# Attention's planned matmuls gathered into every second step, with array shapes counted by the planner

## The chip, the cores and the metric

The kernel runs on one core of one Trainium2 chip. The metric is device time in microseconds (us) of that core; the time before is 1631.56 us, the median of three runs (1630.38 to 1631.83). A profile is one further execution, taken with the hardware profiler.

## The reference

Four sequences of 1024 tokens with 256 channels, all in float32, pass one layer of attention and one mixture of experts:

```
x = x + layernorm(attention(layernorm(x)))   # 16 heads of 16, RoPE on q and k, softmax
x = x + layernorm(moe(layernorm(x)))         # 8 experts, the 2 farthest by distance
                                             # to a centroid, weights softmaxed
```

An expert is silu(x Wg + bg) * (x W1 + b1), times W2, plus b2, with 684 hidden channels. Attention's scores are q k / 4, and its softmax runs over all 1024 keys of a sequence.

## The kernel before, in words

The program has three parts: a start (to about 74 us), attention's steps (to about 1022 us) and the experts (the rest, with a short tail for the last layernorm). The change is in the second.

**Units and steps.** Heads are taken in groups of four. A unit is one sequence, one group of heads and one half of the queries (512); there are 32 units, in the list `order`. A unit has 8 steps, one for each 128 keys, so there are 256 steps, written out by `step(n)` (L709). A step does on TensorE (PE):

- `scores` for two pairs of heads (L723): four products of keys and queries into `sc` (L730), on 64 rows of the array, and four small products that add the negative row maximum `shift` (L736). ScalarE (ACT) takes exp of each into `e` (L740).
- up to three `peaks` (L701), usually two, of a later unit: each is two products `pm` (L645), also on 64 rows, whose row maxima VectorE (DVE) takes into `part` (L648). They run some 12 steps ahead (LEAD, L791). When a unit's maxima are complete, DVE makes `mx` of them (L619 to 624), PE transposes it into `pmx` (L628), and ACT copies that to `shift` (L632).
- `weighted` (L799): the product of the step before's `e` with the values, four matmuls `av` (L805), each on 32 columns of the array.
- then up to QUOTA (L790) planned parts, in the loop of L780.

**Planned parts.** Everything else that attention's part must do is a `Work` (L406): a generator that yields the cost of its next piece and then writes it out. "P540 A550" says that the piece takes 540 ns of PE and then 550 of ACT; D is DVE, G GpSimd (POOL), W a wait only. The Works that use PE put a whole 128 x 128 array to use: transposes `pt`, `ps`, `po`, `ptm`, `pd`, and products `pp`, `pv`, `py`, `pdist`, `rank`. Among them, for the next sequence, `prepare` (L461) normalizes x and `project` (L494) makes q and k (`pp`, copied by ACT to `turned`, L508); `split` (L555) turns q and k by their positions on POOL (`rot`, `sw`) and cuts them into a high and a low half (`split`); `stack` (L565) transposes these (`ps`, L572), copies them by ACT (`half`, L580), and SyncE's queue (SP) copies them by DMA into the tiles `stack` (L592) that pm and sc read.

**The order.** PE, DVE, ACT and SP run their instructions in the order in which the Python program writes them out, and `pool` keeps POOL's in that order too. The program decides it by a plan: `free` holds, for each engine, the time up to which it believes it to be taken. `run_one` (L452) takes the first Work by due time whose next piece fits. A piece fits (L417) when the Works it comes after have been written out to their end, its own time `ready` has come, and no engine would be taken too far ahead (ROOM). `finish` (L446) writes out a Work at once, whether it fits or not; it is called when its result is needed, as for `shifts[u]` at a unit's first step. The plan adds 230 ns of PE for a pair of pm (L705), 460 for a pair of heads' sc (L742), and 1200 for a step's av (L809); a change of the array's shape has no cost of its own in it.

**Banks.** sc and most of the planned parts share a ring of four PSUM banks, which ACT empties; pm, pmx, pd, py, pdist and rank share a ring of three, which DVE mostly empties.

Of the kernel before, what the change touches and what calls it, by code (L numbers as in the profile page):

```python
# [16 lines left out]
P = 128  # L17
# [40 lines left out]
def sandwich(  # L58
# [22 lines left out]
    def bank(name, pool=ps1):  # L81
        return pool.tile([P, TB], F32, tag="bank", name=name)
# [217 lines left out]
    for e in range(NE):  # L300
        for w, to, cols in (
            (wg, 0, slice(0, FF)), (w1, FF, slice(FF - (P - R2), FF)), (w1, FF + P - R2, slice(0, NC * P))
        ):
            n = cols.stop - cols.start
# [84 lines left out]
    free = dict.fromkeys("PDAG", 0)  # L389
# [4 lines left out]
    def bank_free(r, n):  # L394
        return max(ring[r][(taken[r] + i) % len(ring[r])] for i in range(n))

    def take(r, until):
        ring[r][taken[r] % len(ring[r])] = until
        taken[r] += 1

    ROOM = dict(P=10**9, D=1400, A=2600, G=15000)
    LAG = dict(P=280, D=120, A=150, G=200, W=0)
    at_step = [0]
# [2 lines left out]
    class Work:  # L406
# [10 lines left out]
        def fits(self):  # L417
# [6 lines left out]
            if self.ready > (now if first in "PW" else max(now, free[first])):  # L424
                return False
            return all(e == "W" or free[e] + c - now <= ROOM[e] for e, c in costs)

        def run(self):
            t = self.ready
            bank_used = self.need[0] == "P"  # L430
            if bank_used:
                r = self.costs()[1][0]
                t = max(t, bank_free(r, 1))
            for i, (e, c) in enumerate(self.costs()):
                if e != "W":
                    t = max(t, free[e], free["P"] - 300)
                    free[e] = t + c
                t += c + LAG[e]
                if bank_used and i == 1:
                    take(r, t)  # L440
            self.ready = t
            self.need = next(self.gen, None)
            if self.need is None:
                works.remove(self)
# [7 lines left out]
    def run_one(first="PADGW"):  # L452

        w = next((w for w in works if w.need[0] in first and w.fits()), None)
        if w:
            w.run()
        return w
# [198 lines left out]
    def outputs(u, av):  # L656

        b, g, qb = order[u]
        ou = ap2.tile([P, TB], F32, tag="ou", name=f"ou_{u}")
        nc.scalar.copy(ou, av)  # L660
        free["A"] = max(free["A"], free["P"] + 300) + 550
        av_free[0] = free["A"] + LAG["A"]

        def turn_back():
            yield "P500 D750"
            if g == 0:
                old = divmod(b * NQB + qb - 3, NQB)
                if old in closing:
                    closing[old].finish()
                outs[b, qb] = cl.tile(  # L670
                    [P, NTB, NH, HD], F32, tag="outs", name=f"outs_{b}_{qb}", bufs=3
                )
            pd = bank(f"pd_{u}")
            for i in range(NTB):
                nc.tensor.transpose(
                    pd[:, i * P : (i + 1) * P], ou[:, i * P : (i + 1) * P], ident
                )

            by = pd.rearrange("p (t j d) -> p t j d", j=4, d=32)
            rec = small.tile([P, NTB, 4], F32, tag="rec", name=f"rec_{u}")  # L680
            nc.vector.reciprocal(rec, by[..., HD])
            nc.vector.tensor_tensor(
                outs[b, qb][:, :, 4 * g : 4 * g + 4, :], by[..., :HD],
                rec[..., None].to_broadcast([P, NTB, 4, HD]), ALU.mult,
            )

        back = Work(turn_back(), at_step[0] + 5)
        backs.append(back)
        back.ready = av_free[0]
        if g == NG - 1:  # L690

            before_ = list(settling.values())
            closing[b, qb] = Work(
                finish(b, qb), at_step[0] + 6,
                after=[back] + late + [closing[k] for k in closing] + before_[:-1],
            )
            settling[b, qb] = Work(
                settle(b, qb), at_step[0] + 8, after=[closing[b, qb]] + before_
            )

    def peaks():  # L701
        for _ in range(2):
            free["D"] = max(free["D"], free["P"] + 500) + 605
            take("D", free["D"] + LAG["D"])
        free["P"] += 230  # L705
        drawn[0] += 1
        next(tops)

    def step(n):  # L709

        u, kb = n // NT, n % NT
        at_step[0] = n
        b, g, qb = order[u]
        if kb == 0:
            shifts[u].finish()
        es = []
        if bulk and (n % 3 < 2 if n < 53 else n > 60):
            to, of = bulk.pop(0)  # L720
            nc.sync.dma_start(out=to, in_=of)

        def scores(pr):  # L723
            q, k_ = stacks[b, g, qb][pr][0], stacks[b, g, kb // NTB][pr][1]
            kt = kb % NTB * P
            scs = []
            for s in range(2):
                r = slice(64 * s, 64 * s + 64)
                sc = bank(f"sc_{n}_{pr}_{s}", pssc)
                nc.tensor.matmul(  # L730
                    sc, k_[r, kt : kt + P], q[r], start=True, stop=False
                )
                scs.append(sc)
            for s in range(2):
                r = slice(64 * s, 64 * s + 64)
                nc.tensor.matmul(  # L736
                    scs[s], bring[pr][r, :], shift[u][r, :], start=False, stop=True
                )
                e = ap1.tile([P, TB], F32, tag="e", name=f"e_{n}_{pr}_{s}", bufs=8)
                nc.scalar.activation(e, scs[s], AF.Exp, scale=1.0 / HD**0.5)  # L740
                es.append(e)
            free["P"] += 460  # L742
            for s in range(2):
                free["A"] = max(free["A"], free["P"] + 300) + 485
                take("A", free["A"] + LAG["A"])

        def when(kind):
            if kind == "M":
                return bank_free("D", 2)
            if kind == "V":  # L750
                return max(weighted_ready[0], av_free[0] if waiting[0][1] == 0 else 0)
            return bank_free("A", 2)

        lead = min(LEAD, NT + n // 4)
        share = max(0, min(3, 2 * (n + lead) - drawn[0], len(order) * UNIT - drawn[0]))
        todo = ["M"] * min(share, 1) + [0, 1] + ["M"] * (share - 1)
        while todo:
            kind = next((k for k in todo if when(k) <= free["P"] + 100), None)
            if kind == 1 and 0 in todo:
                kind = 0  # L760
            if kind is None:
                if set(todo) == {"M"} and drawn[0] > 2 * (n + NT + 2):
                    break
                if run_one("ADGW"):
                    continue
                kind = min(todo, key=when)
                if kind == 1 and 0 in todo:
                    kind = 0
            free["P"] = max(free["P"], when(kind))
            todo.remove(kind)  # L770
            if kind == "M":
                peaks()
            else:
                scores(kind)
            while run_one("ADGW"):
                pass
        if waiting:
            free["P"] = max(free["P"], when("V"))
            weighted(*waiting.pop(0))
        for i in range(QUOTA):  # L780
            while run_one("ADGW"):
                pass
            if not run_one("P"):
                break
        while run_one("ADGW"):
            pass
        waiting.append((u, kb, es))
        weighted_ready[0] = free["A"] + LAG["A"]

    QUOTA = 2  # L790
    LEAD = 12  # L791
    UNIT = 4 * NTB
    shifts, closing, settling, backs = {}, {}, {}, []
# [5 lines left out]
    def weighted(u, kb, es):  # L799
        b, g, qb = order[u]  # L800
        if kb == 0:
            avs[u] = psav.tile([P, TB], F32, tag="av", name=f"av_{u}")
        av = avs[u]
        for j in range(4):
            nc.tensor.matmul(  # L805
                av[32 * j : 32 * j + 32, :], v_aug[kb][:, 4 * g + j, :], es[j],
                start=(kb == 0), stop=(kb == NT - 1),
            )
        free["P"] += 1200  # L809
        if kb == NT - 1:  # L810
            outputs(u, av)

# [612 lines left out]
    def open_pool(key, stack, **kw):  # L1425
        room[key] = stack.enter_context(tc.tile_pool(name=key, reuse_waits="tile", **kw))
# [11 lines left out]
    def make_room():  # L1438
        attn.close()
        beside[0] = True  # L1440
        ROOM.update(D=3000, A=3500)
        open_pool("psu", behind, bufs=5, space=PSUM)
# [14 lines left out]
    with tc.manual_schedule(engines={ET.SP, ET.PE, ET.DVE, ET.Activation}):  # L1457
# [24 lines left out]
        while waiting:  # L1482
            weighted(*waiting.pop(0))
# [134 lines left out]
```

## Time and profile before

| | us |
|---|---|
| median of three runs | 1631.56 |
| the profiled execution's own time | 1639.77 |
| its span, first to last instruction | 1638.0 |
| attention's steps, 74 to 1022 | 948.0 |
| PE busy in them | 917.1 |
| DVE busy in them | 746.3 |
| ACT busy in them | 681.3 |
| POOL busy in them | 362.3 |

In the trace, a float32 product appears as two matmuls (a step's four av as eight). PE's rows give the time from the start of a group's first matmul to the modelled end of its last, and neighbouring groups overlap a little, so the time of a piece is better read from start to start. A row ends with the idle time of its engine before it, in brackets, and with what ended that. The mean granted clock of PE is 0.976 of full speed over the span, and 1.00 in the steps.

### The profile page before, as it was taken

What the parts mean: (1) busy time and instruction counts of PE and PEld (TensorE: products, weight loads), DVE (VectorE), ACT (ScalarE), POOL (GpSimd) and SP (SyncE); (2) the same over time, 40 slices, a digit from 0 to 9 for tenths busy, and PEclk for the clock granted to TensorE, in tenths of its full rate; (3) what the DMA queues carried; (4) which work ended last, traced back from release to release, by engine and by line L of the source; (5) the groups of instructions that cost most, each with busy time, mean ns of one, the idle gap of its engine ahead of it and who ended that gap; (6) DMA issues with size and microseconds to landing.
All of it is one profiled execution on the core that took longest, in us unless ns stands there. A gap on an engine that the chain in (4) does not pass through costs nothing. (4 is left out here: it accounts for less than half of the span.)

```text
span 1638.0 us, 27716 instructions
## 1 busy us (share of the span) xinstructions
PE 1532.8 (94%) x9456; PEld 1004.4 (61%) x9456; DVE 1046.5 (64%) x2511; ACT 854.8 (52%) x1754; POOL 513.2 (31%) x951
## 2 busy tenths in 40 slices
PE   7889999999999999999999999999999999999960
PEld 4444455645545554445554444788888888899950
DVE  4686788787788787868788883434434433334348
ACT  3366777677777767767677667322311111222213
POOL 6652152254372344462243112133230111111100
PEclk9899999999999999999999999999999999999985
DMA  4299887246054232212141042145455555788855
GB/s 121 90 247 237 236 237 186 85 117 177 12 132 136 75 103 80 53 52 65 37 94 40 1 159 87 66 167 203 179 183 195 195 194 221 251 312 300 304 226 199
DMA packets 114036, 247.94 MB, mean 151 GB/s; under 512 B 16772, under 2 KB 76967, under 8 KB 108007
## 3 DMA queue, kind: packets, MB, share of 16 engines
q1 hardware_dynamic: 103287, 215.47, 42.1%
q0 software_dynamic: 9120, 26.38, 4.9%
q10 hardware_dynamic: 1488, 4.33, 0.7%
q8 instruction: 75, 1.23, 0.3%
q14 instruction: 66, 0.54, 0.1%
HBM read 149.18 MB, written 80.73 MB: 140 GB/s over the span
## 5 line engine op out<-in xcount | busy, mean ns | idle before, releaser
L648 DVE TENSOR_REDUCE part<-pm 128x1 f32<-128x512 f32 x1024 | 640.5, 683 | 134.1 <-PE pm L645 132.1
L740 ACT ACTIVATE e<-sc 128x512 f32<-128x512 f32 x1024 | 530.2, 604 | 149.0 <-PE sc L736 147.5
L1330 PE MATMUL pu<-xT,w 128*128 128x256 f32 (+3 forms) x2024 | 359.9, 333 | 2.4 <-DMA w<-wall 1.2
L1330 PEld LDWEIGHTS pu<-xT,w 128*128 128x128 f32 (+1 forms) x2024 | 313.7, 190 | 33.2 <-issue 1.6
L1336 ACT ACTIVATE sil<-pu,w 128x256 f32<-128x256 f32 (+3 forms) x276 | 117.1, 425 | 415.9 <-PE pu L1330 392.9
L645 PE MATMUL pm<-stack,stack 64*128 64x512 f32 x992 | 282.5, 465 | 15.0 <-DVE part L648 11.9
L805 PE MATMUL av<-e,v 128*32 128x512 f32 x2048 | 274.9, 606 | 0.3 <-ACT e L740 0.3
L1341 DVE SCALAR_TENSOR_TENSOR h<-pu,w,sil 128x256 f32<-128x256 f32 (+1 forms) x230 | 97.2, 423 | 221.5 <-ACT sil L1336 220.6
L645 PEld LDWEIGHTS pm<-stack,stack 64*128 64x128 f32 x992 | 136.5, 185 | 162.1 <-DVE part L648 111.1
L730 PE MATMUL sc<-stack,stack 64*128 64x512 f32 x992 | 220.1, 405 | 4.1 <-ACT half L580 3.6
L736 PE MATMUL sc<-shift,bring 64*128 64x512 f32 x1024 | 222.7, 398 | 0.5 <-ACT shift L632 0.2
L1377 POOL DMA_INDIRECT res<-yo,ids x71 | 68.8, 969 | 411.7 <-DVE yo L1376 406.3
L1364 PE MATMUL pe<-w,h 128*128 128x256 f32 x710 | 167.5, 383 | 0.0
L1364 PEld LDWEIGHTS pe<-w,h 128*128 128x128 f32 x710 | 132.6, 190 | 25.4 <-issue 8.3
L730 PEld LDWEIGHTS sc<-stack,stack 64*128 64x128 f32 x992 | 113.8, 186 | 37.9 <-ACT e L740 15.0
L736 PEld LDWEIGHTS sc<-shift,bring 64*128 64x128 f32 x1024 | 105.7, 185 | 21.4 <-ACT shift L632 5.2
L1376 DVE TENSOR_SCALAR yo<-pe,xt 128x256 f32<-128x256 f32 x71 | 34.4, 484 | 90.3 <-PE pe L1364 90.2
L805 PEld LDWEIGHTS av<-e,v 128*32 128x32 f32 x2048 | 40.8, 108 | 71.1 <-issue 65.5
L992 POOL DMA_INDIRECT rows<-xr,to x64 | 62.6, 978 | 55.9 <-DVE to L987 34.6
L139 POOL TENSOR_TENSOR t_y<-y_y 128x4 f32<-128x4 f32 x24 | 4.7, 197 | 182.2 <-DVE y_y L334 181.0
L503 PE MATMUL pp<-wqk,nT 128*128 128x512 f32 (+1 forms) x128 | 61.1, 604 | 0.0
L139 POOL TENSOR_TENSOR rot<-turned,bias_qk 128x512 f32<-128x512 f32 x30 | 39.2, 1307 | 67.0 <-ACT turned L508 66.9
(297 smaller groups left out, 1396.2 us busy)
## 6 DMA issues: line engine op xcount, KB each, us to landing
w<-wall SPq DMA_DIRECT2D x46, 2034.0 KB
rows<-empty SPq DMA_DIRECT2D x35, 1032.0 KB
stack<-half SPq DMA_DIRECT2D x186, 128.0 KB
stack<-half SPq DMA_DIRECT2D x124, 64.0 KB
xt<-rows SPq DMA_DIRECT2D x25, 258.0 KB
wall<-in_wg_dram SPq DMA_DIRECT2D x16, 342.0 KB
wall<-in_w_dram SPq DMA_DIRECT2D x16, 320.0 KB
wall<-in_w_dram SPq DMA_DIRECT2D x8, 640.0 KB
```

The costliest lines, as they stand in the source:

```text
L645: nc.tensor.matmul(pm, q[r, i * P : (i + 1) * P], k_[r], start=True, stop=True)
L648: nc.vector.tensor_reduce(part[:, i, 2 * pr + s, half : half + 1], pm, AX.X, ALU.max)
L730: nc.tensor.matmul(sc, k_[r, kt : kt + P], q[r], start=True, stop=False)
L736: nc.tensor.matmul(scs[s], bring[pr][r, :], shift[u][r, :], start=False, stop=True)
L740: nc.scalar.activation(e, scs[s], AF.Exp, scale=1.0 / HD**0.5)
L805: nc.tensor.matmul(av[32 * j : 32 * j + 32, :], v_aug[kb][:, 4 * g + j, :], es[j], start=(kb == 0), stop=(kb == NT - 1),)
L992: sent = nc.gpsimd.indirect_dma_start(out=rows[:, :], out_offset=bass.IndirectOffsetOnAxis(ap=to[:, i, t : t + 1], axis=0), in_=xr[:, t, i ...
L1330: nc.tensor.matmul(pu[:m, i, :n], w[:, c0 : c0 + m], xT[:, k, :n], start=(k == 0), stop=(k == KC - 1),)
L1336: nc.scalar.activation(sil[:m, :n], pu[:m, 0, :n], AF.Silu, bias=w[:m, OB + f : OB + f + 1])
L1341: nc.vector.scalar_tensor_tensor(h[:, f, :n], pu[:, 1, :n], bias, sil[:, :n], ALU.add, ALU.mult)
L1364: nc.tensor.matmul(po[:, :C], hs[j % 2][:, f, i * P : (i + 1) * P], w[:, O2 + f * C : O2 + (f + 1) * C], start=False, stop=(f == NC - 1),)
L1377: sent = nc.gpsimd.indirect_dma_start(out=res[:, :], out_offset=bass.IndirectOffsetOnAxis(ap=ids, axis=0), in_=y, in_offset=None,)
```

## The change

The planned parts of a step are taken in even steps only, and then up to four instead of two. The planner keeps the shape in which it last left the array (128, 64 or 32) and adds PE time when a piece needs another: 225 ns for a change to 64, 210 to 32, 150 to 128. In return av costs 860 instead of 1200. The costs of a plain step in the plan are thus 230 x 2 + 460 x 2 + 860 + 225 + 210 = 2675 instead of 2580. No instruction is added or removed; all four engines' orders are decided anew.

```diff
+    shape = [0]
+
+    def array(rows_):
+
+        if rows_ != shape[0]:
+            free["P"] += {64: 225, 32: 210, P: 150}[rows_]
+            shape[0] = rows_
+
...
             if bank_used:
+                array(P)
                 r = self.costs()[1][0]
...
     def peaks():
+        array(64)
...
         def scores(pr):
+            array(64)
...
-        for i in range(QUOTA):
+        for i in range(QUOTA if n % 2 == 0 else 0):
             while run_one("ADGW"):
                 pass
             if not run_one("P"):
...
-    QUOTA = 2
+    QUOTA = 4
...
         av = avs[u]
+        array(32)
         for j in range(4):
...
-        free["P"] += 1200
+        free["P"] += 860
```

In the changed file these lines stand 9 to 12 lines further down.

## Prediction

> **What bounds the kernel now.** First the page's head and its 40 slices (41 us each; a digit is a tenth of busy time), to see which engine is full where.
>
> ```profile
> span 1638.0 us, 27716 instructions
> ...
> PE   7889999999999999999999999999999999999960
> ...
> DVE  4686788787788787868788883434434433334348
> ```
>
> PE is full from the fourth slice to the last but two; DVE has sixes to eights up to slice 25, the end of attention, and threes and fours after it. The change only touches attention's steps, so I took the stretch between the first and the last weighted sum (columns: each engine's busy time and instructions, PE's granted clock, DMA share, GB/s).
>
> ```profile
> 74.00:1022.00 948.00, 917.14 (x6147) 485.23 (x6143) 746.30 (x1594) 681.28 (x1365) 362.28 (x688) 1.00 0.42 115
> ```
>
> 256 steps in 948 us. PE is busy for 917, DVE for 746, ACT for 681. Then the timeline of PE, for what a step is made of (start, duration, operation):
>
> ```profile
> 504.81 1.06 PE L805 MATMUL av<-e,v 128*32 128x512 f32 x8
> 505.81 0.53 PE L572 MATMUL ps<-ident_r,split 128*128 128x128 f32 x4
> 506.27 0.50 PE L645 MATMUL pm<-stack,stack 64*128 64x512 f32 x2
> ...
> 507.98 1.07 PE L805 MATMUL av<-e,v 128*32 128x512 f32 x8
> 508.97 0.50 PE L645 MATMUL pm<-stack,stack 64*128 64x512 f32 x2
> ...
> 510.68 1.06 PE L805 MATMUL av<-e,v 128*32 128x512 f32 x8
> 511.68 0.50 PE L645 MATMUL pm<-stack,stack 64*128 64x512 f32 x2
> ```
>
> A step without a planned part takes 2.70 us (507.98 to 510.68); with one ps it takes 3.17. Nothing in between is idle: the step is PE's. Last, what PE itself waited for in this stretch:
>
> ```profile
> PE pm L645 <- DVE part L648: 10.2, 25, 1.1
> PE pmx L628 <- DVE mx L624: 8.2, 7, 1.5
> PE ps L572 <- POOL split L139: 4.1, 2, 2.4
> ```
>
> These rows miss waits that sit on weight loads. So I took every group of matmuls, start to start, and its excess over the fast quarter of its kind: 867 us of work and 80 us of waiting, of which 33 us and more are pm behind the row maxima (DVE), 8.8 pmx behind its maxima, 4.6 ps behind POOL's split, 6 sc behind ACT's copy of ps.
>
> **Part 1, merged blocks.** A planned part uses the whole 128x128 array, pm and sc 64 rows, av 32 columns. I counted, in the built programs of both kernels, the runs of whole-array work inside the steps: 165 before, 118 after, both with 246 parts (before: 84 single, 81 pairs; after: 48 single, 32 pairs, 18 triples, 20 fours). What a merge saves is read from pairs that already exist, start to start: ps alone 462 ns, ahead of another part 366, last in a run 465, so two single ps cost 924 and a pair 831: 93 saved. pd and ps: 586+462 alone, 412+465 together: 171. pp and ps: 1914+462 against 1420+781: 175. The 47 merges are thus worth 4.4 to 8.2 us; with each part at its own row the sum over all steps gives nearer the lower end, and I take **-5**. A pv and a pc move into the steps from ahead of them, where PE was not full (1.06+0.3 us); a ptm and a pdist leave for the expert stage, where they cost as much. **+1** (0 to +1.4).
>
> **Part 2, DVE's share.** Four reductions take 2.48 us of a plain step's 2.70 (timeline of DVE), so other DVE work in a plain step overruns it. I laid each DVE instruction of both programs, at its row's duration, to the step whose pm follows it. Time by which DVE's sum exceeds PE's: 47.0 us in 36 runs of such steps before, 48.8 in 50 runs after. A lone small surplus costs nothing (a step at 486.2 has 3.02 of DVE and took 2.71); with 0.3 us forgiven per run it is 36.5 before, which is near the measured waits, and 34.4 after. Over eight steps together it is 18.7 and 6.3: before, surpluses stand in rows of up to eleven, after, heavy steps lie between. Ends: +2 and -12. I take **-3**, near the sum that fits the trace.
>
> **Part 3, pmx behind its maxima.** The waits of over 0.9 us came where the last pm was 1.3 to 2.5 us ahead of pmx. With 1.3 us it waited three times out of three, 1.0 to 1.3 us each; the changed program has two such places against three, and fewer with 2.5. I expect 3 to 4 us of 8.8: **-5** (0 to -8).
>
> **Part 4, ps behind the split: the loss.** The planner lets a Work start when those it comes after have been written out (fits, L417), not when they are done; a stack's own ready time is set when it is made. So its ps may be placed as soon as the split has been handed to POOL, which then needs:
>
> ```profile
> 715.91 1.30 POOL L139 TENSOR_TENSOR rot<-turned,bias_qk 128x512 f32<-128x512 f32 x1 [9.18 <-ACT turned L508]
> ...
> 721.49 0.64 POOL L139 CAST split<-rot 128x512 fp32r<-128x512 f32 x1
> 722.21 1.28 POOL L139 TENSOR_TENSOR split<-rot,split 128x512 fp32r<-128x512 f32 x1
> ```
> ```profile
> 720.54 0.66 PE L675 MATMUL pd<-ident,ou 128*128 128x128 f32 x4
> 723.54 0.53 PE L572 MATMUL ps<-ident_r,split 128*128 128x128 f32 x4 [2.35 <-POOL split L139]
> ```
>
> rot takes 5.58 us, the two halves of the split 2.0, and ps starts right after, PE idle for 2.35; at 459.1 it was 1.72. Before, two or three steps lay between the last pp of a batch's second half and that ps. The changed program has, at step 100, in this order on the two engines:
>
> ```
> PE:   pp_1_3, rank, ps_0_0_1 <- split_0_1
> POOL: rot_1_0, rot_0_1 <- turned_1, split_1_0, split_0_1
> ```
>
> With two steps' parts in one, the pp that ends the projection, the split and the ps fall into the same block. From the end of pp: ACT's copy and the hand-over 0.7 (447.2 to 447.92 in the trace), rot 5.6, the other group's split 2.0, its own 2.0: 10.3 us, less 0.44 for rank: PE idle 9.9. If POOL comes late (its y_d chain of 4.95 and rot_1_0 of 5.6 start some 8.6 us before that pp ends) it is 11.2. I take 10.5. Behind the waiting ps stand, on PE's queue, all pm, sc and av; so ACT and DVE run dry as well. Step 164 repeats step 100 instruction by instruction. At step 46 one plain step lies between: 0.7+5.6+2.0 less 5.4 is 2.8. Together 23.8 against 4.1 before: **+20** (+16 to +22). All engines' queues being empty after each, some of part 2's waits go: **-2**.
>
> **What moves at no cost.** A ps is followed on SP by ten copies into the stacks (issued over 6.2 us at 500.67). In the steps of the changed program at least 13.5 us of PE work lie between a ps and the first pm or sc that reads its stack, 16.7 before; it covers the copies, and without it that pm would wait the few us missing. The counts for the expert tables move from step 233 to 242, and the first expert tile's loads behind them on SP; some 24 us of steps still follow, against 61 before (issued 967.3, used 1028.5); 2 MB at the 312 GB/s of the page's best slice is an estimated 7 us, so they cover it, and a rest of at most 2 us is in the range. Two maxima transposes more than before stand alone at a unit's start and hold sc for 0.3 us each; also in the range.
>
> **Part 5, the clock.** The wait at 723.5 left this (granted clock is the third figure from the end):
>
> ```profile
> 721.60:725.00 3.40, 1.46 (x12) 1.30 (x14) 0.81 (x2) 0.59 (x1) 3.24 (x4) 1.00 0.01 2
> 725.00:728.40 3.40, 3.40 (x17) 1.14 (x15) 2.12 (x4) 2.06 (x4) 3.24 (x4) 0.50 0.00 0
> ```
>
> 3.4 us at half clock, in which the groups took 1.4 us longer than usual; the 1.72 wait left none. [...] By the row, 2.35 is enough: 1.4 for the short one, 2.1 for each long one, less 1.4 that goes: **+4.2**. I go by the row; ends 0 and +7.
>
> **Sum.** -5 +1 -3 -5 +20 -2 +4.2 = +10.2. Made against the profiled execution: span 1638.0, own time 1639.77, which is 8.2 above the median of 1631.56; I carry the difference over to the median: about 1642.
>
> **Rivals.** (A) As summed: 1642; for it the order on POOL and PE, which holds whatever the times are. 0.64. (B) The relief of parts 2 and 3 is whole: -12 and -8; then -5+1-12-8+20-2+4 = -2, 1630. For it the eight-step sums; against it the rows of before, where two steps of surplus already stall. 0.12. (C) Faster: the planner's clock, right at 2.68 per plain step where it was 2.58, takes DVE off PE's path altogether: the place is pm behind part, the price its 33 us and more. It decides from a relief of 27 us in parts 2 and 3 together; at 20 and 8.8 the sum is about -11, 1621. Against it: each plain step still has up to 0.8 us of surplus. 0.12. (D) The edit does not do what it says: the shape changes saved are not on the path, since 48 single parts remain and PE then waits for DVE instead; part 1 is nothing, part 2 +2: +20, 1652. 0.12.
>
> **Numbers.** A measurement of this kernel can tell about 0.2%, 3.3 us, from no change. Slower A and D, 0.76; same B, 0.12; faster C, 0.12. The range takes the ends of parts 2, 3 and 5 around A and reaches to B: 1630 to 1652.
>
> **What would show it.** PE's waits for POOL split: near 24 us in three places, two of about 10 with three steps' work after them at half clock. pmx behind mx under 4 us. pm behind part within a few us of before. Steps without parts still 2.70, whole-array runs of 118. I am wrong if POOL had finished those splits early, if the waits are there but the total of pm's waits falls by 20 us, or if the expert stage moves by more than 2 us.

## The result, and the profile after

| | before | after |
|---|---|---|
| median of five runs, us | 1631.56 (1630.38 to 1637.47) | 1660.16 (1656.11 to 1661.61) |
| ratio | 1 | 1.0166, 95% interval 1.0153 to 1.0179 |
| the profiled execution's span | 1638.0 | 1659.8 |
| first weighted sum to the last of the scores (start to start) | 947.1 | 974.6 |
| first weighted sum to the last matmul of the last one | 950.6 | 979.5 |
| half-clock time of PE within these | 3.4 | 44.4 |

The change costs 28.6 us. The forecast was slower by 10.4, in a range that ended at 1652: the direction was right, the size and the range were not. All of it is in attention's steps: they are 27.5 us longer up to the last scores, 28.9 up to the end of the weighted sums, and the time from there to PE's last matmul is 556.0 us in both. The profiled execution of before had spent some 7 us more than after's in the start, ahead of the steps, which is why the spans differ by 21.8 only and the medians by 28.6.

The page after, head and slices:

```profile
span 1659.8 us, 27713 instructions
...
PE   7889999999979998979999999999999999999960
```

The 26-slice stretch of attention now has sevens and eights in PE's row (slices 12, 16, 18), where it was nines. The stretch of the steps (columns as before):

```profile
67.00:1047.00 980.00, 922.23 (x6157) 489.28 (x6155) 755.83 (x1594) 681.54 (x1364) 361.02 (x688) 0.98 0.41 110
```

980 us for the same 256 steps, of which PE was busy 922, so 58 idle where there were 31. PE's waits from 70 to 1060:

```profile
PE ps L581 <- POOL split L139: 24.9, 3, 11.0
PE pm L654 <- DVE part L657: 19.9, 27, 2.6
PE pmx L637 <- DVE mx L633: 4.5, 2, 3.3
```

The first row was 4.1 us, the second 10.2, the third 8.2. The split waits are where the prediction put them; here is the second of the two long ones, PE and then POOL:

```profile
719.63 1.98 PE L512 MATMUL pp<-wqk,nT 128*128 128x512 f32 x4
721.45 0.30 PE L976 MATMUL rank<-both,above 128*128 128x32 f32 x2
721.59 0.39 PE L979 MATMUL rank<-run,ones 128*128 128x32 f32 x2
732.95 0.75 PE L581 MATMUL ps<-ident_r,split 128*128 128x128 f32 x4 [10.97 <-POOL split L139]
```
```profile
718.13 1.31 POOL L139 TENSOR_TENSOR rot<-turned,bias_qk 128x512 f32<-128x512 f32 x1
...
723.58 1.26 POOL L139 TENSOR_TENSOR rot<-turned,bias_qk 128x512 f32<-128x512 f32 x1
...
729.66 1.29 POOL L139 TENSOR_TENSOR split<-rot,split 128x512 fp32r<-128x512 f32 x1
```

POOL still had the other group's rot to finish (from 718.13), then this one's (from 723.58), then two splits: the late case of the prediction, 11.0 rather than 10.5.

As in the prediction, I then took every group of PE, start to start, and its excess over the fast quarter of its kind, and put it down to the last releaser within it (the operation whose end let PE go on):

| us | before | after | difference | forecast |
|---|---|---|---|---|
| work (fast quarter of each kind, summed) | 867.4 | 858.1 | -9.3 | -4 (part 1) |
| pm behind part (DVE) | 33.3 | 44.0 | +10.7 | -3, and -2 of part 4 |
| pmx behind mx | 8.8 | 4.6 | -4.2 | -5 (part 3) |
| ps behind split (POOL) | 4.6 | 25.3 | +20.7 | +20 (part 4) |
| everything else, half clock included | 33.0 | 42.6 | +9.6 | +4.2 (part 5) |
| sum | 947.1 | 974.6 | +27.5 | +10.2 |

Two terms were sized well, one gave more than I had allowed, and two lost more: DVE's, of the wrong sign, and the rest. The rows depend somewhat on which groups count as one kind. With kinds set by the group before, the group behind and the number of matmuls, and fast quarters common to all kernels, the work falls by 7.1 and pm's row grows by 11.2; the pmx and ps rows stay as they are.

### The profile page after: what moved, and what is told of

Its sections match the earlier page's. It is cut to its first block, busy times and chain, and to the rows that moved or that the text cites. A ratio compares the mean times of both kernels' runs of the same rounds, so it can differ in the third digit from the quotient of the medians.

```text
span 1659.8 us, 27713 instructions
## 1 busy us (share of the span) xinstructions
PE 1527.6 (92%) x9456; PEld 1003.2 (60%) x9456; DVE 1056.2 (64%) x2511; ACT 854.5 (51%) x1754; POOL 511.8 (31%) x951
## 5 line engine op out<-in xcount | busy, mean ns | idle before, releaser
L589 ACT CAST half<-ps 128x512 fp32r<-128x512 f32 x62 | 36.8, 599 | 51.3 <-PE ps L581 50.7
L581 PE MATMUL ps<-ident_r,split 128*128 128x128 f32 x256 | 37.3, 274 | 25.7 <-POOL split L139 24.9
```

## Theories

Theory 1: the three split waits and the half clock behind them carry the loss. Theory 2: gathering the parts leaves DVE's work to the plain steps (those without parts), so that DVE sets the pace, and the split waits only stand where PE would have waited for DVE. Theory 3: the new costs, not the gathering, moved the works for the worse. The kernels below were run in four sets of four, in this order; each ratio is to runs of the kernel before on the same chip, and the second set's chip was slower (before took 1655.92 us there), so sets are compared by ratio.

## First set: the two halves of the change, and the ready times

Ready times are one edit in `fits`, on the changed kernel:

```diff
-            if self.ready > (now if first in "PW" else max(now, free[first])):
+            ready = max([self.ready] + [w.ready for w in self.after])
+            if ready > (now if first in "PW" else max(now, free[first])):
```

**After with ready times.**

> The changed kernel, and a Work now also waits until the Works it comes after are ready, not only written out; so each ps stands three to six steps behind the pp that its split needs. Theory 1 (the three waits of ps for POOL's split and the half clock behind them carry the loss): 25.3 us of waits fall to under 5, and the eight half-clock stretches of 3.4 us behind them (some 1.5 us each) go: -22 - 12, about 1626 us. Rival, theory 2 (gathering the parts makes the steps between them DVE's, and the long waits only stand where PE would have waited for DVE): pm's waits for part rise above their 44 us as the split waits go, and the time is 1640 to 1650.

Measured: 1635.72, ratio 1.0027 (1.0018 to 1.0037), 24.4 us below the changed kernel.

```profile
PE pm L655 <- DVE part L658: 15.5, 25, 1.7
PE pmx L638 <- DVE mx L634: 7.8, 8, 1.2
PE pm L655 <- DMA stack<-half: 5.7, 2, 4.3
```

No split row is left. pm's excess is 41.7 against 44.0, so it did not take the split waits' place: theory 2 is wrong in that. But the gain is 24 and not 34, and a wait is new: pm for the copies into the stack. I come back to both.

**New costs alone** (on the changed kernel: the loop takes QUOTA parts after every step, and QUOTA is 2).

> The planner's counts of shape changes alone (array, 860 for av), two parts after every step as before the change. 161 runs of whole-array work, no ps behind its own pp in one step. Theory 1: no long wait, 1629 to 1634 us, as before the change. Theory 2: also as before, since nothing is gathered. Rival, theory 3 (the new costs move DVE's and POOL's works against PE and make the pm waits): 1640 or more, with pm's waits near 44 us rather than 33.

Measured: 1639.21, ratio 1.0048 (1.0025 to 1.0072), slower than theory 1 wanted. pm's excess is 34.6, against 33.3 before, so theory 3's reason is not there. What is there is a split wait that I had not seen in the order: 7.8 us at one place (step 98), where two rotations, which POOL runs interleaved, and the split stand ahead of it:

```profile
PE ps L581 <- POOL split L139: 9.5, 3, 7.8
```

**Gathering alone** (on the kernel before: `range(QUOTA if n % 2 == 0 else 0)`, QUOTA 4).

> Up to four parts after every second step alone, with the planner's old costs. 122 runs of whole-array work; in two steps the pp that ends a half, and the ps that needs its split, stand together. Theory 1: two split waits of about 8 to 10 us each and their half clock, 1650 to 1660 us. Theory 2: pm's waits of 44 us as with the whole change, so also slow; told apart by the rows. Theory 3: 1632 to 1642.

Measured: 1650.92, ratio 1.0116 (1.0099 to 1.0133), in theory 1's range. Split waits 20.5 us in three places (8.7 twice), pm 46.7.

**New costs and ready times, two parts after every step.**

> The new costs with two parts after every step, and the ready times of the Works before as in the first kernel. Theory 1: the 4.1 us of split waits before the change go, with one half-clock stretch: 1625 to 1631 us. Theory 2: as the kernel with the new costs alone, less those 4 us. If it is slower than the first kernel by over 3 us, gathering the parts is worth something on its own.

Measured: 1620.06, ratio 0.9936 (0.9918 to 0.9954): the fastest of all kernels that compute the whole, below both kernels of the comparison. It is 15.7 us faster than the gathered kernel with the same costs and ready times. So the gathered order loses something beyond the split waits.

```profile
PE pm L655 <- DVE part L658: 11.7, 19, 1.7
...
PE pmx L638 <- DVE mx L634: 1.3, 2, 0.8
```

## Second set: DVE out of the way

On each of four kernels:

```diff
-                            part[:, i, 2 * pr + s, half : half + 1], pm, AX.X, ALU.max
+                            part[:, i, 2 * pr + s, half : half + 1], pm[:, : TB // 2], AX.X, ALU.max
```

> The kernel before, with each row maximum taken over the first 256 of the 512 scores only (the maxima of the others are left out), so that DVE's four reductions of a step take about 1.4 us rather than 2.48 and DVE stands ahead of PE in every step; PE's order is unchanged. By the waits' rows, pm's 33 us and pmx's 8.8 go: about 1590 us, and pm behind part under 3 us. It is the measure for the next kernel.

> The changed kernel with the same halved maxima. Theory 1 (split waits and their half clock carry the loss; DVE's waits add 11): it loses its 44 us of pm's waits and 4.6 of pmx's, about 1610, so 20 us over the kernel before with halved maxima: 20.7 of split waits and 8 to 12 of half clock, less 9 of merged blocks. Theory 2 (DVE is what the gathering costs): the two are within 10 us. If merging is worth nothing, the two are 30 apart.

> The changed kernel with the ready times of the Works before and halved maxima: neither split waits nor DVE's. What is left against the kernel before with both edits is the merged blocks: theory 1, 8 to 9 us below it, 1578 to 1582 if that has 1588. If the two agree within 3 us, the merges are worth nothing on the path.

> The kernel before with the ready times of the Works before and halved maxima: 4.1 us of split waits and one half-clock stretch less than with halved maxima alone, 1584 to 1590 us. Against the kernel before with halved maxima it gives what the ready times are worth without DVE; against the one ahead of it, what gathering is worth.

| halved maxima | us | ratio | pm behind part | ps behind split |
|---|---|---|---|---|
| before | 1609.61 | 0.9717 (0.9681 to 0.9753) | 8.1 | 5.5 |
| after | 1632.03 | 0.9850 (0.9818 to 0.9881) | 19.8 | 24.3 |
| before, ready times | 1601.27 | 0.9659 (0.9621 to 0.9696) | 12.7 | 0 |
| after, ready times | 1607.38 | 0.9704 (0.9669 to 0.9739) | 18.2 | 0 |

After is over before by 22.4 us with halved maxima, 1.4% (about 0.9 to 1.9 from the two intervals), against 1.66% with whole ones. That is theory 1's 20, and it says that most of the loss doesn't need DVE at its limit; whether it shrank at all the intervals don't tell. The halved reductions left pm waits of 8 to 20 us, more than I expected, and more in the gathered kernels.

With ready times as well, I expected the gathered kernel 8 to 9 us below the other, since only the merged blocks would be left. It is 6 us above (0.5% plus or minus 0.5). By my rows its work is 830.3 against 844.0, 14 us less; but the other kernel's stretch holds one weighted sum more (1.0), and with fast quarters common to the two it is 3 us less (836.8 against 839.9). So some of the merges' saving is there, and its size is not known. The waits eat it: they are 12 us more by the second count, of which 6.0 are pm's waits for the copies into the stack, which the other kernel doesn't have. My reading of part 1 as a saving that stays was wrong.

## Third set: the half clock, POOL and the old costs

**Before with ready times.**

> The kernel before with the ready times of the Works before alone (old costs, two parts after every step). It closes the square: with it, gathering and the new costs can each be priced with the split waits gone. If the new costs by themselves lose 8 us, as without the ready times (1639 against 1632), this is about 1612; if what they lost there was only the split wait of 7.8 us that their order had made, this is 1620 to 1626, as the kernel with costs and ready times (1620).

Measured: 1631.02, ratio 0.9989 (0.9975 to 1.0003): no difference that can be told, and 1620 to 1626 was missed (one split wait of 2.0 us stays in this order). With ready times, then, the new costs are worth 0.9936/0.9989, -0.5%; without them they lost 0.5%; that this was the one split wait of 7.8 us and what hung on it is argued.

**After with PE kept busy in the waits.**

```diff
+            idle = {(1, 0, 1): 24, (2, 0, 1): 100, (3, 0, 1): 100}.get((b, g, half), 0)
+            for _ in range(0 if is_k else idle):
+                nc.tensor.transpose(ps[:, :P], ident_r, ident_r)
             for t in range(NTB):
```

> The changed kernel with 24, 100 and 100 extra transposes of the identity (some 92 ns each) ahead of the three ps that wait for POOL's split, into the bank that ps then writes: PE waits as long as before, but is not idle. Order and all else unchanged. If the half clock after those waits has a price of its own (eight stretches of 3.4 us, 1.5 us each), 10 to 13 us fall away, about 1648. Rival: after such a wait ACT and DVE have to refill anyway, and the half clock is covered by them: within 3 us of 1660.

Measured: 1657.86, ratio 1.0162 (1.0137 to 1.0187), against 1.0166. The two cannot be told apart: the price of 10 to 13 us is refuted, for these places. It is no test of half clock everywhere. In the steps 27.3 of the 44.4 us at half clock are left, with 26.0 us of PE's work in them where it was 29.5, because stretches came at 78.5 and 95.6, near the start, while others went. The stretch after the second long wait, in the changed kernel (granted clock is the third figure from the end):

```profile
726.00:736.20 10.20, 3.25 (x16) 2.37 (x16) 1.68 (x5) 1.42 (x3) 6.58 (x7) 0.50 0.00 0
```

10.2 us at half clock; but PE was waiting until 732.95, so 6.95 of them lay in the wait itself, and only 3.25 us of PE's work ran in the rest. From ps to the next av it took 3.45 us (732.95 to 736.40); the filled kernel, whose granted clock was 1.00 from 725 to 735:

```profile
720.50 8.80 PE L582 MATMUL ps<-ident_r 128*128 128x128 f32 x100
731.80 0.53 PE L584 MATMUL ps<-ident_r,split 128*128 128x128 f32 x4 [2.50 <-POOL split L139]
...
733.97 1.07 PE L820 MATMUL av<-e,v 128*32 128x512 f32 x8
```

2.17 us, so the half clock's price was 1.28 here, and the next step gave 0.4 of it back, waiting for DVE (0.43 <- part at 737.12). At the first of the long waits the filled kernel still fell to half clock, after an idle time of 2.57 us:

```profile
471.00:477.80 6.80, 6.22 (x28) 3.31 (x30) 3.43 (x10) 2.65 (x5) 0.52 (x1) 0.50 0.00 0
```

Over the steps around all three places it saved 1.5 us: 2.3 at step 46 and 0.7 at step 164, less 1.5 at step 100.

**After with ready times, without the rotation.** In `rotated`, the lines from `sh = ...` to the last add run only `if e is not pool`.

> The changed kernel with the ready times of the Works before, and without the rotation on POOL (turned plus bias goes straight to the split; the two products, the two in-place steps are left out), so POOL's 5.6 us per split are 1.3; PE's and DVE's order unchanged. It is the kernel of 1635.7 us, 1.0027 of before, with POOL off DVE's back. If DVE's stretched small works (1.1 us for 0.17 while POOL ran rot) make the added pm waits, pm behind part falls from 41.7 us to about 32, 1.5 to 1.0 half-clock stretches go, ratio 0.995. Rival (DVE's works come clumped because PE's parts do): pm stays over 38 us and the ratio over 1.000.

Measured: 1630.07, ratio 0.9992 (0.9978 to 1.0006). pm behind part 39.9 against 41.7: the first expectation (32) is refuted, and here the operations left out are not what makes pm wait. That clears the rotation, not POOL. At steps 80, 82 and 95 three small operations of DVE for the choice of experts (over, p and gt) take 0.67, 0.95 and 1.28 us beside POOL's split and xb, where their usual times are 0.17, 0.16 and 0.42, and pm's longest waits for DVE, 0.7 to 1.5 us, stand there and at the same works 64 steps later. The 5.7 us it is faster by are 1.8 there, some in the stack copies (3.8 against 5.5), and fewer half-clock stretches (10.4 us against 20.5); I did not take them further apart.

**New costs, ready times, up to four in any step.**

> New costs and ready times, and up to four parts after every step, not only every second: parts stand together only where that many are due (155 runs of whole-array work against 166 with two). If merging helps where nothing has been held back for it, 1 to 2 us less than two per step, 1618. If four parts together cost more in waits than the merges save, as between the first and the fourth kernel of the first set (+15.7), it is slower than 1620 by up to 5.

Measured: 1627.58, ratio 0.9968 (0.9948 to 0.9988), slower than the 1620 with two. Two pmx waits of 3.0 us, both with the same blocks around them (steps 102 and 166), are most of the difference (0.3%, some 5 us by the ratios):

```profile
PE pmx L638 <- DVE mx L634: 8.3, 4, 2.9
...
452.66 3.27 DVE L633 CAST mx<-m 128x16 fp32r<-128x16 f32 x1
```

The second line is the cast ahead of the first of them. It takes 0.18 us elsewhere. Here POOL runs four operations without a pause from 452.62 to 455.89, and the cast ends with the last of them. So this difference need not be a price of four parts in a step.

## Fourth set: the same order with a faster POOL, and parts that come late

**Gathering and ready times, old costs.**

> Up to four parts after every second step and the ready times, with the old costs. If the rest of the loss is gathering's own, it is as slow against its neighbour with two parts after every step (0.9989 of before) as the kernel with the new costs is against its own (1.0027 against 0.9936): about 1.007, 1643 us. If the rest came from the new costs' order, it is near 0.999, 1630.

Measured: 1658.64, ratio 1.0168 (1.0143 to 1.0192). More than expected: gathering costs 1.8% here. The row that grew most is not pm behind part (41.6 against 39.1) but the stack's; pmx behind mx grew too, from 4.1 to 11.3, of which 5 us are one wait (step 110), where the two operations on mx take 2.99 and 2.50 us beside POOL's rotation:

```profile
PE pm L646 <- DMA stack<-half: 16.9, 6, 4.5
...
PE pmx L629 <- DVE mx L625: 10.9, 6, 5.0
```

**After without the rotation, order untouched.**

> The changed kernel without the rotation on POOL (the two products and the two in-place steps are left out), every engine's order unchanged. From pp to ps the chain is then 0.7 + 1.3 + 2.0 + 2.0 less 0.4, 5.6 us, in place of 11.1, twice, and the third wait goes: the split waits fall from 25.3 to about 11. If a microsecond of such waits is a microsecond of time: -14, about 1.0080 of before. If they only stand where PE would have waited for DVE anyway: within 5 us of 1660, and pm's waits rise above 50.

Measured: 1638.53, ratio 1.0042 (1.0029 to 1.0055), 20 us below the changed kernel rather than 14. The split waits are 11.5 us, as worked out:

```profile
PE pm L655 <- DVE part L658: 15.3, 27, 1.5
PE ps L582 <- POOL split L139: 11.1, 2, 5.5
```

That is 13.8 less, and pm's excess fell by 5.7, from 44.0 to 38.3: together 19.5 of the 20.2 us (1.24% of 1631.7). A microsecond of these waits is a microsecond of time, within the 3 us that the intervals leave open. Where the 5.7 come from can be read in DVE's timeline. The changed kernel at 400 us, DVE and then POOL:

```profile
400.28 1.05 DVE L356 TENSOR_SCALAR var_m<-mv_m 128x4 f32<-128x4 f32 x1
401.37 0.17 DVE L333 TENSOR_SCALAR i_m<-var_m 128x4 int32<-128x4 int32 x1
401.57 1.12 DVE L334 TENSOR_SCALAR y_m<-i_m 128x4 int32<-128x4 int32 x1
402.60 2.47 DVE L657 TENSOR_REDUCE part<-pm 128x1 f32<-128x512 f32 x4
```
```profile
400.03 1.28 POOL L139 TENSOR_TENSOR rot<-rot,turn 128x512 f32<-128x512 f32 x1
401.38 1.28 POOL L139 TENSOR_TENSOR rot<-rot,sw 128x512 f32<-128x512 f32 x1
```

Two small operations end when POOL's end (401.33 and 401.31, 402.69 and 402.66), and pm waits 2.55 us. In the kernel without the rotation POOL is idle at that point, and the same two lines take 0.17 each:

```profile
395.39 0.17 DVE L356 TENSOR_SCALAR var_m<-mv_m 128x4 f32<-128x4 f32 x1
395.60 0.17 DVE L333 TENSOR_SCALAR i_m<-var_m 128x4 int32<-128x4 int32 x1
395.80 0.17 DVE L334 TENSOR_SCALAR y_m<-i_m 128x4 int32<-128x4 int32 x1
```

There pm waits 0.73. The place comes twice (steps 85 and 149, an excess of 2.9 us each). Why these operations take longer beside POOL's is not shown. The reductions of pm are not stretched there (in the kernel before, four in 2.48 us from 503.63, with POOL's sw from 503.53, and four in 2.48 from 520.79, with POOL idle).

**Before without the rotation.**

> The kernel before without the rotation on POOL: its two split waits of 1.8 and 2.6 go, and POOL's hold on DVE's small works: 4 to 6 us less, about 0.997 of before. If it loses 10 us or more, POOL's share in DVE's waits was large before too.

Measured: 1624.16, ratio 0.9946 (0.9931 to 0.9961), 7.5 us faster, pm 32.4 against 33.3. But pmx behind mx fell from 8.8 to 3.2: the waits at steps 7, 22, 38 and 102, 5.6 us together, are gone. Step 22 in the kernel before, and then the same place without the rotation:

```profile
160.03 1.29 POOL L139 TENSOR_TENSOR rot<-rot,sw 128x512 f32<-128x512 f32 x1
160.19 1.17 DVE L623 CAST mx<-m 128x16 fp32r<-128x16 f32 x1
162.19 0.51 PE L628 MATMUL pmx<-ident_r,mx 128*128 128x128 f32 x4 [1.30 <-DVE mx L624]
```
```profile
159.84 0.18 DVE L624 CAST mx<-m 128x16 fp32r<-128x16 f32 x1
160.47 0.54 PE L629 MATMUL pmx<-ident_r,mx 128*128 128x128 f32 x4
```

So in the old order, too, small works of DVE took longer beside POOL's (1.17 us here, 0.18 without the rotation), but those ahead of pmx and hardly those ahead of pm. The pair after to before is now 14.4 us apart instead of 28.6. Of the 14.2 less, the rows give 9.8 to split waits (11.5 and 0.6 are left), 4.8 to pm and 4.7 to groups without a releaser; pmx takes 5.7 back, since its gain of 4.2 is now a loss of 1.5.

**After with ready times, three parts in place of four** (QUOTA 3).

> New costs, ready times, and up to three parts after every second step rather than four: 125 runs of whole-array work, DVE's works less clumped, but parts come later; in the first batch the two ps of group 0 stand right before the pm that reads their stack. If gathering loses by holding parts back: pm waits for the copies into the stack there for 8 to 12 us (5.7 with four), and it is slower than the kernel with four (1.0027 of before) by 3 to 8 us. If it loses by clumping: faster than 1.0027 by 3 us or more, pm behind part under 38 us.

Measured: 1657.59, ratio 1.0154 (1.0130 to 1.0179): 1.3% slower than with four, more than the 3 to 8 us that I expected of parts held back. Step 57 shows it. The two ps of a stack have come so late that they are written out right ahead of their pm:

```profile
276.84 0.94 PE L582 MATMUL ps<-ident_r,split 128*128 128x128 f32 x8 [0.37 <-ACT e L752]
286.84 0.80 PE L655 MATMUL pm<-stack,stack 64*128 64x512 f32 x2 [9.06 <-DMA stack<-half]
```

and SP then takes 6.7 us to issue the ten copies:

```profile
279.16 6.67 SPq L602 DMA_DIRECT2D stack<-half  x10
```

In all, 20.4 us of waits for the stack (5.7 with four) and 6.0 for a split. pm behind part is 39.5 against 41.7: fewer parts at once did little for DVE.

## Why the prediction was wrong, step by step

**Part 4, right.** 23.8 us of split waits were forecast, 25.3 came, in the three places and for the reason given (the short one is 2.9 by its own terms and was 3.0). The runs without the rotation show that each microsecond of them counts: 13.8 of them gone, with 5.7 of pm, made 20. Its rider was wrong: the queues, empty after such a wait, were to take 2 us off pm's waits, and nothing shows that they did.

**Part 3, right in size, and partly by luck.** -4.2 against -5. The reason given, the distance from the last pm to pmx, can hold for the three waits of before that stay without the rotation (steps 158, 214 and 238, 3.2 of the 8.8 us). The other four, 5.6 us, are gone without the rotation; at step 22, one of them, the cast to mx took 1.17 us beside POOL's rot and 0.18 without it. The changed order has two waits: one of the first kind (1.3 us), and one of 3.3 at step 7, where an operation on mx takes 2.08 us beside POOL's DMA issue and rot. The sum had no term for either meeting.

**Part 2, the step that failed.** That "heavy steps lie between" was read from DVE's durations in the trace of before, and gave -3. The rows give +10.7. About half of it, 4.8 us, is shown by taking work away: the changed order puts DVE's var_m and y_m under POOL's rot, where they take 1.05 and 1.12 us instead of 0.17; 4.8 is the difference of pm's excess between the two kernels with and without the rotation. The sum used durations of the old order, in which those works did not meet.

The other 5.9 stay without the rotation (38.3 against 32.4). No run takes them away, but the traces show where most of them lie. In the changed kernel without the rotation, 5.3 us of pm's waits stand at steps 3, 74 and 138. There bvs takes 1.34 us (0.28 in the kernel before, ahead of the steps) and d 1.17 and 1.18 (0.18 elsewhere), beside what POOL still has to do; at step 74:

```profile
347.81 1.34 POOL L139 TENSOR_TENSOR split<-rot,split 128x512 fp32r<-128x512 f32 x1
348.02 1.17 DVE L929 TENSOR_SCALAR d<-d 128x32 f32<-128x32 f32 x1
```

The kernel before without the rotation has 2.0 us of such waits. In the changed kernel itself, six steps with a DVE operation stretched in this way (3, 74, 75, 85, 138 and 149) hold 12.7 of pm's 44.0 us; before, three (73, 98 and 162) hold 3.2 of 33.3. That is 9.5 of the 10.7 by position; the cause is shown for 4.8 of them, and for the rest it is read from the rows. With halved maxima the gathered kernels still wait 5 to 12 us more, which I did not take apart. That DVE's works come in clumps is argued only; gathering by threes left pm nearly where it was.

**Part 1, saved more and kept less.** The work fell by 9.3 us (7.1 by the other sorting), where I took 4: the merges and the clean ends of 47 fewer runs. But the second set shows that such a saving need not reach the end: 3 to 14 us of less work there came out as 6 us more time.

**Part 5, right in size where it looked.** I took 2.1 us for each long wait and 1.4 for the short one. The 1.4 is the row's; the 2.1 was my estimate, and no run shows it. By the rows, groups in the half-clock stretches that no releaser explains exceed by 1.3, 1.2 and 1.6 us behind the three waits. The filled kernel shows 1.3 at one place, partly given back, 2.3 at the short wait of 3.0 us, and no total that can be measured. The 44.4 us at half clock look like a large loss and led me to 12 us in the first set's expectation; of the 10.2 us at each of the two long waits, 6.7 and 6.95 passed before the wait had ended (473.33 and 732.95).

**The rest, a term that was missing.** The "else" row grew by 9.6: groups with no releaser in the trace (+8, or +9 by the other sorting), sc behind shift, e, nT and oT (+7), less sc behind half (-4) and smaller ones. Of these I had only the clock behind the split waits. By the other sorting, the groups without a releaser have 9.0 us of excess in half-clock stretches (0.4 before) and 11.7 outside them (11.3 before), so the clock is all of their growth. But only 4.1 of the 9.0 stand behind the three split waits. The other 4.8 stand behind four waits for DVE: 3.28 us of pmx (at 96.68) and 2.55, 2.06 and 2.51 of pm (at 403.34, 615.08 and 663.00), with 6.8, 3.4, 3.4 and 3.4 us at half clock behind them, and each with a DVE operation that took longer beside POOL's (an operation on mx 2.08 us, y_m 1.12, d 1.30, y_m 1.11, where 0.17 or 0.18 is usual). How much of it reaches the end is not shown.

**Rivals and range.** D came nearest: 1652 with DVE at +2, and with DVE's measured 10.7 it would have been 1661. Its other half, that the merges save PE nothing, is not what the rows show; other waits took the place of what they saved. I let DVE's term end at +2, on the strength of a sum that could not see what the new order makes two engines do at once; that is what made the range too narrow.

**What gathering costs.** Against its neighbour with two parts after every step it loses 1.2% with either costs and without ready times, and with ready times 0.9% (new costs) and 1.8% (old). Without ready times the chain from pp over POOL to ps is too short. With them, ps comes so late in places that the copies into the stack are: 17 us of pm's waits with the old costs, 5.7 with the new. Half the steps for parts means that each of the links can wait up to a step more. Not all of these differences are gathering's, though: each kernel is one order, and in each, other small works of DVE happen to meet POOL's. In the kernel of 1620 us pmx waits only 1.4 us for mx, in its neighbours with ready times 8.3 (gathered) and 8.7 (four in any step). Differences of 7 us between two orders can be that alone; the 15 to 29 us here are more. The version to keep is the one that doesn't gather: new costs and ready times, 1620 us.

## What to carry to other kernels

When planned work is given fewer places, follow each chain of works across engines (here PE, ACT, POOL, PE, SP, PE) and ask whether its links still have the time between them that the old spacing gave for nothing; a planner that knows "written out" but not "done" can't see it. A sum of durations from the old trace holds only for pairs of instructions that already ran beside each other: for a new order, give a term for works that now meet, upwards too, and look first at small DVE operations beside POOL's long ones (0.17 us became 1.05 and 1.12 here). Ask of half-clock time how much of PE's work ran in it: at the second long wait 3.25 us in 10.2, at a price of 1.28.

## What the runs showed of the hardware

A tensor_scalar of 128 x 4 took 1.05 and 1.12 us beside POOL's tensor_tensor of 128 x 512 (the changed kernel at 400.28 and 401.57), and 0.17 with POOL idle (without the rotation, at 395.39 and 395.80). A cast of 128 x 16 took 0.18 in the kernel before without the rotation (159.84), 1.17 beside one such operation (the kernel before, 160.19), and 3.27 when POOL ran four operations without a pause (up to four parts in any step, 452.66): it ended with the last of them (455.93 and 455.89).

After an idle time of 2.57 us the clock was 0.50 for 6.8 us in one place, after 2.06 us for 3.4 in another, and after 2.50 it stayed at 1.00 in a third (the filled kernel at 471, the changed kernel at 616.8, the filled kernel at 732).
